# A routed feed-forward that gathers by an inverted list, first projections in two strands, and the next layer's first entry moved forward

## The chip, the cores and the metric

The kernel runs on one core of one Trainium2 chip. The engines of the core work side by side, each through its own queue of instructions in order: PE (matrix products into PSUM), DVE (elementwise work, scans, reductions), ACT (functions and copies), POOL (general work, and the issue of indirect transfers) and SP (issue of transfers). Semaphores order them. The metric is the time of one execution in microseconds (us). The median of three runs of the kernel before is 2760.29 us (2757.69 to 2765.39).

## The reference, cut to what matters

Two layers act on x of 8 batches × 512 tokens × 256 features, in 32-bit floats.

Layer 0 norms x to xn and adds two branches to x. The first is a recurrence over tokens. With dx the difference between a three-tap filter of xn and xn, five mixtures of xn and dx are projected to r, k, v, the gate g and the decay w. For 16 heads of 16 rows a state S of 16 × 16 is run over the tokens forwards and backwards:

```
S = exp(w)[:, None] * S + k[:, None] * v[None, :]      y_t = r_t S     (forwards)
y_t = r_t S;   S = exp(w)[:, None] * (S + k v)                         (backwards)
```

Both sums are gated, normed by head, multiplied by silu(g) and projected by Wo. The second branch is a mixture of 8 experts: each token's two best experts by score (xn Wg^T) compute silu(x W1^T) * (x W2^T) W3^T with 704 hidden values, and the two results are added with the scores as weights.

Layer 1 norms the sum, adds a global (causal) and then a local (window of 64) attention with 16 heads, and a feed-forward of 16 routed experts, four for each token out of two of four groups, beside a shared one.

## The kernel before, in words

**Layer 0, head.** `norm_and_route(b)` (L279) norms a batch, transposes it (xT), writes the transposed batch to DRAM (`lines`), and scores and picks its two experts. `projections(b)` (L480) loads the transposed batch (xnT), forms dx, and makes in one chain: the sigmoid gate (sig), the mixing factors (t5), the mixtures (`mixed`, L551, tile xf) and the projections v, k, r, d (decay), dq (what the two-sided scan multiplies by) and g. The product v goes to DRAM (vd). A plain loop adds the eight routings, two turns for each, and the first projections, entered up to three times in one turn. `clear_slots` (L272) writes zeros over all of `slots`, a DRAM table of 9984 rows of 1 KB (39 chunks of 256). `place` (L311) counts the picks of each expert, gives every pick a row in the table (`slot`), with chunks of 256 rows that belong to one expert, and names the expert of each chunk (`wrow`).

**Layer 0, scans.** `scans` (L674) goes through 128 steps (8 batches × 2 halves × 8 pairs of value rows). A step multiplies v, spread over partitions by eight transfers (`spread`, tile kv), by k (L688), runs two pairs of scans on DVE (L699, L703), multiplies by r (L708), and PE sums over rows (ys, L714). Beside it run the projections of the next batch, `ending` (L726: gate, norm, Wo, and the write of the batch to `after`), and the experts: `scatter` (L372) sends 4096 token rows twice to their slots by 64 indirect transfers from POOL, and `experts` (L410) goes through the 39 chunks: weights by indirect load (`weights`), the chunk's rows by a direct load (`load_slots`, L394), their transpose (xsT, L405), the products, and a write to `outs`.

**Layer 1.** `entry(b)` (L891) loads `after`, gathers for each token its two rows of `outs` (tile y, L903), adds them with weights (L911), norms, transposes, and routes. `heads_of`, `attentions`, `divided` and `ffn` do the attention and the feed-forward; the weights w1 of the feed-forward and of the projections are loaded at its start.

**What sets the order.** Every piece is a Python generator. `Turns.turn` advances each running generator by one step, so a `yield` says how far pieces are interleaved; scans have 4 steps for each of 128, a chunk of experts has 12. PE, DVE, ACT and SP keep this written order (`PINNED`); POOL's order is made by the scheduler. Tiles with one tag share buffers, and a new tile waits until the old one's readers are done.

Of the kernel before, what the change touches and what calls it, by code (L numbers as in the profile page):

```python
# [26 lines left out]
F32 = mybir.dt.float32  # L27
# [33 lines left out]
G1 = 4  # L61
# [13 lines left out]
for _n, _w in (  # L75
    ("ident", P), ("take", 32 + 24), ("mean", P), ("center", P), ("tri8", E0 * E0),
    ("before", P), ("fresh", E0 * NTT), ("full", T * B // CH), ("chunk", NCH), ("part", 1),
    ("tri16", E1 * E1), ("tri4", G1 * G1), ("causal", P), ("band", P + WIN),
    ("cos_g", NT * HD), ("sin_g", NT * HD), ("cos_l", NT * HD), ("sin_l", NT * HD),
):  # L80
    _C[_n] = (_at, _at + _w)
    _at += _w
# [4 lines left out]
def constants():  # L87
# [19 lines left out]
    put("chunk", np.arange(NCH)[None, :])  # L107
# [58 lines left out]
def two_layers(ctx: ExitStack, tc: tile.TileContext, a: dict, out: bass.AP):  # L166
# [6 lines left out]

    cst = const.tile([P, FIRST_L1], F32, name="cst")
# [6 lines left out]
    act_e.dma_start(wg0, a["wg0"])  # L181

# [23 lines left out]
    def layer_norm(dst, src, tag):  # L206
# [8 lines left out]
        rsqrt(rs, rs, NT)  # L215
        for t in range(NT):
            vec_e.tensor_scalar(
                dst[:, t, :], src[:, t, :], mv[:, t, 0:1], rs[:, t : t + 1], ALU.subtract, ALU.mult
            )

    def chosen(dst, s, n, k, tri, tmp, tag, tags=None):

        rows = s.shape[1]
        tags = tags or (f"gt{n}", f"eq{n}")
        gt = tmp.tile([P, rows, n, n], F32, tag=tags[0], name=f"gt{n}_{tag}", bufs=1)
        eq = tmp.tile([P, rows, n, n], F32, tag=tags[1], name=f"eq{n}_{tag}", bufs=1)
# [10 lines left out]


    with ExitStack() as l0:
# [3 lines left out]
        ew = l0.enter_context(tc.tile_pool(name="ew", bufs=2))  # L243
        hpool = l0.enter_context(tc.tile_pool(name="h0", bufs=4))
        ex = l0.enter_context(tc.tile_pool(name="ex", bufs=2))
# [20 lines left out]
        score = keep.tile([P, NTT, E0], F32, name="score")  # L266
        pick0 = keep.tile([P, NTT, E0], F32, name="pick0")
        slots = dram.tile([NSLOT, D], F32, name="slots", bufs=1)
        lines = [dram.tile([D, T], F32, name=f"xnT{b}", tag=f"xnT{b}", bufs=1) for b in range(B)]
        xns = [ex.tile([P, NT, D], F32, name=f"xn{b}", tag=f"xn{b}", bufs=1) for b in range(B)]  # L270

        def clear_slots():  # L272

            zero = rw.tile([P, D], F32, tag="t5a", name="zero")
            vec_e.memset(zero, 0.0)
            n = NSLOT // P
            nc.sync.dma_start(slots.rearrange("(p n) d -> p n d", p=P), bc(zero, 1, n))

        def norm_and_route(b):  # L279
            xn = xns[b]  # L280
            layer_norm(xn, xn, f"a{b}")
# [13 lines left out]
            ps = ps_rw.tile([P, T], F32, tag="rw", name=f"sc_{b}")  # L295
# [9 lines left out]
            chosen(pick0[:, b * NT : (b + 1) * NT, :], s, E0, TOP0, C["tri8"], rw, f"a{b}")  # L305
# [4 lines left out]

        def place():  # L311
            def tmp(shape, name, tag=None):
                return rw.tile(shape, F32, tag=tag or name, name=name, bufs=2 if tag == "gn" else 1)
# [9 lines left out]
            pe.matmul(ps[:, 1, :], one, flat(pick0), start=True, stop=True)  # L323

# [15 lines left out]
            vec_e.tensor_tensor(past, bc(C["chunk"], 2, E0), bc(chto, 1, NCH), ALU.is_ge)  # L340
# [4 lines left out]
            vec_e.tensor_copy(wrow, own)  # L345

# [17 lines left out]
            vec_e.tensor_copy(slot[1], high)  # L364
            vec_e.tensor_tensor(at, pos, bc(high, 2, E0), ALU.is_equal)
# [6 lines left out]
        def scatter():  # L372
            for n in range(NTT):
                for i in range(2):
                    put = pool_e.indirect_dma_start(
                        out=slots,
                        out_offset=bass.IndirectOffsetOnAxis(ap=slot[i][:, n : n + 1], axis=0),
                        in_=xns[n // NT][:, n % NT, :], in_offset=None,
                    )

                    tc.declare_no_dep(put.ins, group="scatter", query=mybir.DependencyQuery.ANY_SYNC, reason="slots are disjoint")
                    tc.add_to_no_dep_group("scatter", put.ins)
                yield

# [9 lines left out]
        def load_slots(i):  # L394
            xs = ex.tile([P, NS, D], F32, tag="xs", name=f"xs_{i}", bufs=2)
            pool_e.dma_start(
                xs, slots[i * CH : (i + 1) * CH].rearrange("(n p) d -> p n d", p=P)
            )
            return xs
# [10 lines left out]
        def experts():  # L410
            nxt = weights(0, "wgu", a["w0_gu"], GU0, 2)
            ps = turned(0, load_slots(0))
# [67 lines left out]
        def projections(b):  # L480

            xnT = rw.tile([P, NC, T + 2 * PAD], F32, tag="xnT", name=f"xnT_{b}")
            pool_e.memset(xnT[:, :, 0:PAD], 0.0)
            pool_e.memset(xnT[:, :, PAD + T :], 0.0)
            nc.sync.dma_start(
                xnT[:, :, PAD : PAD + T], lines[b].rearrange("(c p) t -> p c t", p=P)
            )
            xT = [xnT[:, c, PAD : PAD + T] for c in range(NC)]
            for _ in range(3):
                yield  # L490

            def shifted(c, s):
                return xnT[:, c, PAD + s : PAD + s + T]
# [7 lines left out]
            def project(w, xs, co, name):  # L501
# [8 lines left out]

            dx = big("dx", 1)
            for c in range(NC):
                o = dx[:, c, :]
                vec_e.tensor_scalar(o, xT[c], V("conv1", c), None, ALU.mult)
                vec_e.scalar_tensor_tensor(o, shifted(c, -1), V("conv0", c), o, ALU.mult, ALU.add)
                vec_e.scalar_tensor_tensor(o, shifted(c, 1), V("conv2", c), o, ALU.mult, ALU.add)
                yield
            dxs = [dx[:, c, :] for c in range(NC)]

            sig = big("sig")  # L520
            pss = []
            for co in range(NC):
                pss.append(project(5, dxs, co, f"gate{co}"))
                yield
            for co in range(NC):
                act_e.activation(sig[:, co, :], pss[co], AF.Sigmoid, bias=V("gate_b", co))
            xxx = []
            for c in range(NC):
                t = rw.tile([P, T], F32, tag="xf", name=f"xxx{c}_{b}", bufs=4)
                vec_e.scalar_tensor_tensor(t, dxs[c], V("maa_x", c), xT[c], ALU.mult, ALU.add)  # L530
                xxx.append(t)
# [3 lines left out]
            yield  # L535
            both = ((t5a, 0, 0, P), (t5b, P, 64, 96))
            pss = []
            for _, lo, r0, r1 in both:
                ps = bank(f"t5{lo}")
                for c in range(NC):  # L540
                    pe.matmul(
                        ps[r0:r1, :], m1w[:, c, lo : lo + r1 - r0], xxx[c],
                        start=c == 0, stop=c == NC - 1,
                    )
                pss.append(ps)
                yield
            for (t5, _, r0, r1), ps in zip(both, pss):
                act_e.activation(t5, ps[r0:r1, :], AF.Tanh)
            yield

            def mixed(*fs):  # L551

                xs = {f: [] for f in fs}
                for c in range(NC):
                    pss = []
                    for f in fs:
                        ps = bank(f"m{f}{c}")
# [8 lines left out]
                    for f, ps in zip(fs, pss):  # L566
                        t = rw.tile([P, T], F32, tag="xf", name=f"xf{f}{c}_{b}", bufs=4)
# [3 lines left out]

                        (vec_e if b < 2 else pool_e).tensor_tensor(t, t, xT[c], ALU.add)
# [5 lines left out]
            def projected(xs, w, name):  # L578

                pss = []  # L580
                for co in range(NC):
                    pss.append(project(w, xs, co, f"{name}{co}"))
                    yield
                return big(name), pss

            xv, xk = yield from mixed(2, 1)
            v, pss = yield from projected(xv, 2, "v")
            for co in range(NC):
                act_e.copy(v[:, co, :], pss[co])
            vd = dram.tile([D, T], F32, tag="vd", name=f"vd_{b}")  # L590
            act_e.dma_start(vd.rearrange("(c p) t -> p c t", p=P), v)
            yield


            k, pss = yield from projected(xk, 1, "k")
            for co in range(NC):
                act_e.mul(k[:, co, :], pss[co], -1.0)
            yield

            d = rw.tile([P, NC, T + 1], F32, tag="d", name=f"d_{b}", bufs=2)  # L600
            vec_e.memset(d[:, :, T:], 0.0)
            dT = d[:, :, :T]
            xw, xr = yield from mixed(0, 3)
            ps = bank("dw")
            for c in range(NC):
                pe.matmul(ps[:64, :], dw1[:, c, :], xw[c], start=c == 0, stop=c == NC - 1)
            yield
            act_e.activation(th[:64, :], ps[:64, :], AF.Tanh)
            r, pss = yield from projected(xr, 0, "r")
            for co in range(NC):  # L610
                act_e.copy(r[:, co, :], pss[co])
            pss = []
            for co in range(NC):
                pss.append(bank(f"w{co}"))
# [809 lines left out]
```

## Time and profile before

| what | value |
|---|---|
| median of three runs | 2760.29 us |
| the profiled execution's own time | 2747.16 us |
| its span, first to last instruction | 2745.4 us |
| PE, DVE busy | 2338.7 us (85%), 2141.9 us (78%) |
| ACT, POOL busy | 865.9 us (32%), 472.3 us (17%) |
| first product of the scans, last one's end | 144.86 us, 1443.7 us |
| first matmul of layer 1's feed-forward | 1513.5 us |
| HBM read and written | 215.17 MB, 45.88 MB |

A row of the profile's table of stretches gives the stretch, its length, and for PE, PE's weight loads, DVE, ACT and POOL the busy time with the number of instructions, then the granted clock of PE, the share of DMA and its GB/s. A row of the timeline gives the start, the time, the engine, the line, the operation and its tiles; in brackets stands the idle time before it and what ended it. A row of the waits gives who waited for whom: us in all, times, longest.

### The profile page before, as it was taken

To read this page: it belongs to the slowest core of one execution; us is meant where nothing else is said; L and a number is where in the kernel's file an instruction comes from. 1 tells how busy PE (TensorE), PEld (TensorE's weight loads), DVE (VectorE), ACT (ScalarE), POOL (GpSimd) and SP (SyncE) were. 2 spreads that over 40 slices of the span, in tenths; PEclk is the share of its full clock that TensorE was granted. 3 is DMA by queue.
4 is the path that set the end of the run, shared out by engine and by line. 5 is a ranking of instruction groups with operands and counts; after the bars stand their busy time and mean duration, and the time that the engine had idled before them with its cause. 6 is when DMAs were issued, how large, how long until landed. Compare 5 with 4: busy or idle time off the path is not lost. (4 is left out here: it accounts for less than half of the span.)

```text
span 2745.4 us, 32489 instructions
## 1 busy us (share of the span) xinstructions
PE 2338.7 (85%) x11772; PEld 1392.8 (51%) x11772; DVE 2141.9 (78%) x3042; ACT 865.9 (32%) x1649; POOL 472.3 (17%) x446
## 2 busy tenths in 40 slices
PE   4756897998989889898864899999989989998996
PEld 3313555555555555555632445555545545555554
DVE  4698989989999999999994857667576676666666
ACT  1303231232312323132111344444333444334344
POOL 0075132222223222132202110010010101001000
PEclk8767998989999999998986999999989999999998
DMA  8245555445454454545533100010010111000000
GB/s 286 77 147 167 149 162 163 132 135 158 157 174 133 140 161 142 175 153 153 174 87 140 55 28 24 9 45 21 16 32 32 31 32 31 22 26 20 20 9 16
DMA packets 108912, 263.23 MB, mean 96 GB/s; under 512 B 25265, under 2 KB 56401, under 8 KB 103633
## 3 DMA queue, kind: packets, MB, share of 16 engines
q1 hardware_dynamic: 76304, 119.35, 15.1%
q0 software_dynamic: 23616, 124.14, 13.9%
q10 hardware_dynamic: 8832, 17.65, 1.7%
q8 instruction: 95, 1.56, 0.2%
q14 instruction: 65, 0.52, 0.1%
HBM read 215.17 MB, written 45.88 MB: 95 GB/s over the span
## 5 line engine op out<-in xcount | busy, mean ns | idle before, releaser
L703 DVE TENSOR_TENSOR_SCAN kv<-d,kv 128x512 f32<-128x512 f32 x256 | 336.9, 1316 | 8.8
L699 DVE TENSOR_TENSOR_SCAN kv<-dq,kv 128x512 f32<-128x512 f32 x256 | 324.8, 1269 | 2.5
L426 PE MATMUL g<-xsT,wgu 128*128 128x256 f32 x936 | 248.0, 412 | 20.1 <-ACT xsT L418 19.6
L465 PE MATMUL y<-wdn,h 128*128 128x256 f32 x936 | 254.5, 410 | 8.7 <-DVE h L435 8.7
L1167 ACT ACTIVATE pt_g<-sc_g 128x512 f32<-128x512 f32 (+1 forms) x384 | 171.0, 532 | 236.4 <-PE sc_g L1159 201.7
L426 PEld LDWEIGHTS g<-xsT,wgu 128*128 128x128 f32 x936 | 188.3, 206 | 102.1 <-issue 38.6
L465 PEld LDWEIGHTS y<-wdn,h 128*128 128x128 f32 x936 | 170.8, 197 | 105.2 <-issue 73.7
L1261 PE MATMUL g<-xT,w 128*128 128x512 f32 x384 | 197.5, 639 | 24.8 <-DVE h L1296 9.4
L1261 PE MATMUL u<-xT,w 128*128 128x512 f32 x384 | 190.7, 620 | 18.7 <-DVE h L1296 7.6
L714 PE MATMUL ys<-kv,cst 128*32 128x512 f32 x512 | 123.2, 653 | 79.0 <-DVE kv L708 78.8
L426 PE MATMUL u<-xsT,wgu 128*128 128x256 f32 x780 | 189.3, 382 | 0.0
L1307 PE MATMUL y<-w,h 128*128 128x256 f32 x768 | 179.3, 385 | 0.0
L426 PEld LDWEIGHTS u<-xsT,wgu 128*128 128x128 f32 x780 | 148.2, 191 | 36.2 <-issue 14.0
L708 DVE TENSOR_TENSOR kv<-kv,r 128x1024 f32<-128x1024 f32 x128 | 160.2, 1251 | 3.7
L1279 DVE TENSOR_TENSOR h<-h,u 128x512 f32<-128x512 f32 x96 | 66.0, 688 | 123.6 <-PE u L1261 119.0
L688 DVE TENSOR_TENSOR kv<-kv,k 128x1024 f32<-128x1024 f32 x128 | 160.2, 1251 | 0.0
L1307 PEld LDWEIGHTS y<-w,h 128*128 128x128 f32 x768 | 141.7, 190 | 32.2 <-issue 9.5
L452 ACT ACTIVATE h<-g 128x512 f32<-128x512 f32 (+1 forms) x117 | 61.5, 526 | 300.6 <-PE g L426 300.3
L1173 DVE TENSOR_TENSOR pt_g<-pt_g,cst 128x512 f32<-128x512 f32 x128 | 85.2, 686 | 69.7 <-ACT pt_g L1167 69.6
L1167 ACT ACTIVATE pt_l<-sc_l 128x384 f32<-128x384 f32 (+1 forms) x256 | 98.0, 470 | 90.9 <-PE sc_l L1159 72.9
L1261 PEld LDWEIGHTS g<-xT,w 128*128 128x128 f32 x384 | 71.4, 199 | 107.2 <-issue 82.6
L903 POOL DMA_INDIRECT y<-outs,slot x64 | 64.7, 1010 | 324.8 <-DVE acc L911 312.6
(298 smaller groups left out, 3858.9 us busy)
## 6 DMA issues: line engine op xcount, KB each, us to landing
kv<-vd SPq DMA_DIRECT2D x1024, 64.0 KB, 2.4
cb<-cd SPq DMA_DIRECT2D x128, 128.0 KB, 2.9
slots<-zero SPq DMA_DIRECT2D x1, 9984.0 KB
xs<-slots POOLq DMA_DIRECT2D x39, 256.0 KB, 7.2
outs<-ys POOLq DMA_DIRECT2D x39, 256.0 KB, 5.7
w<-in_w ACTq DMA_DIRECT2D x12, 384.0 KB, 9.7
xn<-in_x SPq DMA_DIRECT2D x8, 512.0 KB
xnT<-xT ACTq DMA_DIRECT2D x16, 256.0 KB, 2.0
```

Of the source, the lines that this page charges most:

```text
L426: pe.matmul(o, w[:, at + c * P : at + (c + 1) * P], xT[:, c, :], start=c == 0, stop=c == NC - 1,)
L465: pe.matmul(y[:, n, :], hs[j // 2][lo:, j % 2, n * P : (n + 1) * P], wd[lo:, j * D : (j + 1) * D], start=j == 0, stop=j == NJ0,)
L688: vec_e.tensor_tensor(kv, kv, bc(kc, 1, NV), ALU.mult)
L699: vec_e.tensor_tensor_scan(out=kv[:, i, :], data0=qc, data1=kv[:, i, :], initial=0.0, op0=ALU.mult, op1=ALU.add,)
L703: vec_e.tensor_tensor_scan(out=kv[:, i, ::-1], data0=dc[:, ::-1], data1=kv[:, i, ::-1], initial=0.0, op0=ALU.mult, op1=ALU.add,)
L708: vec_e.tensor_tensor(kv, kv, bc(rc, 1, NV), ALU.mult)
L714: pe.matmul(y[r0 : r0 + 32, :], C["take"][:, 24 - 8 * at : 56 - 8 * at], kv[:, i, :], start=at == 0, stop=at == 3, skip_group_check=True,)
L1167: act_e.activation(pt[:, i, :end], scs[i][:, :end], AF.Exp, scale=0.25)
L1173: vec_e.tensor_tensor(pt[:, :, a0 : a0 + m], pt[:, :, a0 : a0 + m], bc(mask[:, :m], 1, 4), ALU.mult,)
L1261: pe.matmul(ps, w[:, k, c * P : (c + 1) * P], xT[:, c, :], start=c == 0, stop=c == NC - 1,)
L1279: vec_e.tensor_tensor(hs[-1], hs[-1], u, ALU.mult)
L1307: pe.matmul(y[:, i, :], hs[k][:, (t + i) * P : (t + i + 1) * P], w1[j - 5 + k][:, 2, :], start=k == 0, stop=k == 5,)
```

## The change

- **The table by gather.** `clear_slots`, `slots` and `scatter` go. `norm_and_route` writes the normed batch as it is to a DRAM tensor `normed`, eight transfers of 512 KB on SP's queue. `turn_round` makes from `slot` the inverse list `whose` (which token stands in a row of the table): each slot is split into its low seven bits and the rest, DVE compares both with a count (128 × 512 and 128 × 312 elements at a time), ACT scales one of the two by the token's number, and 64 matmuls add all up in PSUM. `load_slots` then gathers a chunk's 256 rows from `normed` by two indirect transfers. Rows without a pick get token 0.
- **Place beside the scans.** `place`, `turn_round` and `experts` are one generator that starts with the scans.
- **Two strands.** `projections` returns three generators: `inputs` (dx, t5), `values` (sig, v, k) and `decays` (r, d, dq, then g). For batch 0 the last two run side by side, the second with PSUM banks and tiles of its own; the head ends when k and dq are ready, and g comes after. For the other batches they run one after the other. The add of xn in `mixed` is POOL's for all batches (before: DVE's for batches 0 and 1).
- **The first entry.** When the experts are done, `begin` gives their SBUF space to the weights of layer 1 (w1, gq, go, lqkv), loads them, and starts `entry(0)` beside the last scans. `entry` and its helpers move ahead of layer 0, its tiles into a pool `hold` that both layers share (xn lies there first, then the comparisons of `turn_round`).

```
-        slots = dram.tile([NSLOT, D], F32, name="slots", bufs=1)
+        normed = dram.tile([B * T, D], F32, name="normed", bufs=1)
...
         def norm_and_route(b):
             xn = xns[b]
-            layer_norm(xn, xn, f"a{b}")
+            yield from layer_norm(xn, xn, f"a{b}")
+            nc.sync.dma_start(tokens(normed[b * T : (b + 1) * T]), xn)
             yield
...
-        def scatter():
-            for n in range(NTT):
-                for i in range(2):
-                    put = pool_e.indirect_dma_start(
-                        out=slots,
-                        out_offset=bass.IndirectOffsetOnAxis(ap=slot[i][:, n : n + 1], axis=0),
-                        in_=xns[n // NT][:, n % NT, :], in_offset=None,
-                    )
...
+        def turn_round():
...
+            for k in range(NTT // 4 + 1):
+                if last:
+                    for j in range(4):
+                        for i in range(2):
+                            pe.matmul(
+                                inv, last[0][:, i, j, :], last[1][:, i, j, :],
+                                start=k == 1 and i + j == 0,
+                                stop=k == NTT // 4 and (i, j) == (1, 3),
+                            )
+                    last = None
+                if k < NTT // 4:
+                    ls = held(k % 4, [P, 2, 4, P], f"ls{k}")
+                    hs = held(4 + k % 4, [P, 2, 4, n2], f"hs{k}")
+                    for i in range(2):
+                        for o, of in ((ls, low), (hs, high)):
+                            n = o.shape[3]
+                            vec_e.tensor_tensor(
+                                o[:, i], bc(of[i][:, 4 * k : 4 * k + 4], 2, n),
+                                bc(C["count"][:, :n], 1, 4), ALU.is_equal,
+                            )
+                    for j in range(4):
+                        n = 4 * k + j
+                        act_e.activation(
+                            hs[:, :, j, :], hs[:, :, j, :], AF.Copy, scale=number[:, n : n + 1]
+                        )
+                    last = ls, hs
+                yield
+            vec_e.tensor_copy(whose, inv)
...
         def load_slots(i):
             xs = ex.tile([P, NS, D], F32, tag="xs", name=f"xs_{i}", bufs=2)
-            pool_e.dma_start(
-                xs, slots[i * CH : (i + 1) * CH].rearrange("(n p) d -> p n d", p=P)
-            )
+            for n in range(NS):
+                at = i * NS + n
+                pool_e.indirect_dma_start(
+                    out=xs[:, n, :], out_offset=None, in_=normed,
+                    in_offset=bass.IndirectOffsetOnAxis(ap=whose[:, at : at + 1], axis=0),
+                )
...
-        first = projections(0)
+        start, values, decays = projections(0)
+        beside = [start, values, decays]
         for b in range(B):
             turns.add(norm_and_route(b))
+            if 2 <= b < 8:
+                turns.add(beside[{2: 0, 3: 0, 4: 2, 5: 1, 6: 2, 7: 1}[b]])
             turns.turn()
-            if b == 1:
-                turns.add(first)
-                turns.turn()
-                clear_slots()
-            elif b in (2,3):
-                turns.add(first)
+        while ("scans", 0) not in done:
             turns.turn()
-        for _ in range(3):
-            turns.turn()
-        place()
-        turns.finish()
-        turns.add(then(scatter(), experts()))
+        def begin():
+            side.close()
+            pool = ctx.enter_context(tc.tile_pool(name="w1", bufs=1, side="right"))
+            yield
...
+            turns.add(entry(0))
+            for _ in range(6):
+                yield
...
+            for j in range(NF1):
+                w1.append(pool.tile([P, 3, D], F32, name=f"w1_{j}", tag=f"w1_{j}"))
+                act_e.dma_start(w1[j], a["w1"][j])
+                yield
...
+        slot_work = then(place(), turn_round(), experts(), last())
+        turns.add(slot_work)
         for _ in scans(turns):
             turns.turn()
         turns.finish()
```

## The prediction

> **What bounds the kernel now.** I read first the busy tenths over the span, then the busy time by stretches that I cut at the ends of the stages, then the waits and the order of instructions at the three seams. The stretches (columns: PE, PE weight load, DVE, ACT, POOL busy, then granted clock, DMA share, GB/s):
>
> ```profile
> 0.00:144.86 144.86, 84.39 (x272) 49.32 (x272) 85.10 (x232) 30.65 (x43) 12.93 (x21) 0.80 0.54 183
> 144.86:236.00 91.14, 48.00 (x96) 13.89 (x96) 88.53 (x90) 15.16 (x21) 72.26 (x64) 0.69 0.43 148
> 236.00:249.00 13.00, 7.97 (x28) 5.38 (x28) 1.60 (x3) 4.82 (x6) 3.40 (x4) 0.68 0.65 232
> 249.00:1421.00 1172.00, 1040.46 (x4037) 654.28 (x4036) 1107.29 (x1096) 303.32 (x477) 282.36 (x236) 0.95 0.51 152
> 1421.00:1443.70 22.70, 5.69 (x12) 0.52 (x12) 22.28 (x19) 0.00 (x0) 0.77 (x1) 0.52 0.03 12
> 1443.70:1513.50 69.80, 28.93 (x90) 17.29 (x91) 28.62 (x70) 10.40 (x19) 17.38 (x20) 0.62 0.39 138
> 1513.50:1600.00 86.50, 74.29 (x336) 38.87 (x336) 69.49 (x155) 29.94 (x60) 18.24 (x18) 0.92 0.20 59
> 1600.00:2650.00 1050.00, 976.27 (x6142) 563.11 (x6141) 681.09 (x1290) 427.37 (x920) 62.97 (x82) 0.97 0.08 25
> ```
>
> Three bounds follow each other. The head (to 144.86, the first product of the scans) is a chain: DVE works 85 of 145 us. The scan stage (144.86 to 1443.7, 1298.8 us) is DVE's: 97%, then 94%, then 98% busy. Layer 1 from 1513.5 on is PE's, 93% busy. Between lies a seam of 70 us where nobody works half the time. Two stalls stand in the head and at the first expert chunk (waits from 20 to 145 us; then DVE's and PE's instructions in order):
>
> ```profile
> DVE xf L568 <- PE m L561: 17.5, 3, 15.3
> ...
> ACT t5a L548 <- DMA slots<-zero: 10.6, 1, 10.6
> ```
> ```profile
> 236.12 1.21 DVE L688 TENSOR_TENSOR kv<-kv,k 128x1024 f32<-128x1024 f32 x1
> 248.73 0.75 DVE L568 SCALAR_TENSOR_TENSOR xf<-m,vecs,dx 128x512 f32<-128x512 f32 x1 [11.40 <-PE m L563]
> ```
> ```profile
> 241.03 1.11 PE L405 MATMUL xsT<-cst,xs 128*128 128x128 f32 x4 [17.66 <-DMA xs<-slots]
> ```
>
> The tanh waits until the 10 MB clear has read its source tile; and at 236 the matmul that DVE needs stands in PE's queue behind the transpose of the first gathered chunk, which waits for all 64 scatters. The last seam, in PE's order:
>
> ```profile
> 1460.04 1.99 PE L777 MATMUL o<-wmix,z 128*128 128x256 f32 x8 [0.78 <-DVE x L782]
> 1490.93 2.25 PE L858 MATMUL x<-cst,x 128*128 128x128 f32 x8 [28.89 <-DVE x L926]
> ...
> 1513.50 3.62 PE L1261 MATMUL g<-xT,w 128*128 128x512 f32 x4
> ```
>
> PE has no work of layer 1 until entry(0) has gathered, normed and routed.
>
> **What the skill says.** The Trainium skill, SBUF — State Buffer, "SBUF: two separate sides": DVE and GpSimd share one port pair by an exclusive lock, which a DVE instruction with two SBUF inputs also takes against a GpSimd operation that reads SBUF. The trace agrees: the POOL add of L572 runs from 1.08 to 2.14 us (median 1.92), and the scan of L703, 1.225 at the median, reaches 2.11. The skill, Perfetto Trace Analysis, "Sequencer Loop": an instruction waits in its engine's queue for its semaphores; the 17.66 us above is such a wait, with everything behind it late. The skill, DMA: Bandwidth & Descriptors, "Anatomy of one DMA": about 2.0 us plus bytes over 436 GB/s, so 2.3 us for 128 rows of 1 KB; the trace has 2.8 for y<-outs,slot, which I use.
>
> **The change part by part.** Sums are against the profiled execution (span 2745.4, time 2747.2); the median of the runs shown, 2760.3, stands 13.1 us above it, and I carry the difference over to that median.
>
> 1. Head. place() leaves it: DVE's first instruction of it that waited is at 133.90, the first product at 144.86. The clear leaves it (from 47 to 59 DVE did nothing: 12 us). The gather's source is written by eight 512 KB writes of xn on SP's queue, each waiting for its norm; the load of xnT stands behind two of them, whose norms end near 16 us, before its own data (about 19): no cost. The two strands overlap the values' matmuls with the decays' chain. I walked DVE's new order with old durations: norm statistics 2.4 us a batch, norm 1.4, choice 2.6, dx 2.0 a half, xxx 1.4. Up to 20 us nothing changes (the first xT copy waits for ACT's table at 15.3, the first score for that). From there DVE has, before the strand's first xf: norms 2 to 6, statistics 3 to 6, choices 0 to 3, dx and xxx, together 5×1.4 + 4×2.4 + 4×2.6 + 5.4 = 32.4, so xf near 52; with statistics 7, choice 4 and four xf of 0.74 the fourth ends near 60. The adds go to POOL: four at 1.9 end near 64. Then dw 1.9, tanh 0.6, sc, r, xt, r and v on PE (about 10), w 2.3, table load and exponentials 3.6, so q begins near 81; q 1.9, logarithm and exponential with two loads 5.0 behind the copies of v (about 88); dq 5.1, k 1.2: first product near 94 by full-clock matmuls. (Its kv: vd issued near 83, 3.0 to land, eight issues of 0.45 and 2.4 to land, 92; SP's last normed write, ahead of them, waits only for norm 7 near 62.) The granted clock was 0.57 to 0.64 in parts of the old head; I add 6 for it: **100**, so **−45** (−55 to −35). Check from the other side: the old chain without place (−15), clear (−12) and the g input (−3) gives 115, and the strands must hide some 15.
> 2. place() on DVE beside the scans, which DVE bounds: **+11** (133.90 to 144.86 without a gap). The first strand's xf of g after the first product: **+1.5**.
> 3. turn_round: 16 comparisons 128x512, 16 of 128x312, 9 small. The rows 128x512 (L228) are 0.69 long and start 0.60 to 0.72 apart; 128x312 (L340) is 0.48. 16×0.65 + 16×0.46 + 1.9 = **+19.7** (17 to 24). Its 64 matmuls and 32 ACT scalings lie where PE is 53% and ACT 17% busy: hidden; uncovered, each group of eight would hold DVE for about 2 us.
> 4. The 64 scatters (POOL busy 73 us) go, and with them the 11.4 us stall; list and first gather can leave a stall of 0 to 8, I take 4: **−7.4**. Each chunk has two indirect gathers of about 1.3 us on POOL instead of one direct issue of 0.74; POOL is 24% busy and its new order has the gathers two chunks ahead: nothing. If that lead went, PE would wait as at 241. On POOL the first gather waits for the list, and adds of batch 1 queue behind it; batch 1's scans need those only some hundred us later.
> 5. Batch 1's ten adds go from DVE (0.69 each) to POOL: −6.9, given back in part by the shared lock: **−5**.
> 6. entry(0) moves into the last 25 turns of the scans, where DVE is full: 8 accumulations 3.9, statistics and norm 3.9, routing 13.2: **+21**. Its gathers wait for the last chunk's outs (5.7 us to land), then 1.3 apart and 2.8 to land, with a second group behind the first; DVE's accumulations stand ahead of the last scans, which stand still with them: the ys copy to the fourth landing is 0.6 + 0.8 + 5.7 + 3×1.3 + 1.0 + 2.8 = 15 us, DVE's own work in between about 12; the second group needs 8 and finds 4. So 7, and 1 for routing behind ACT's weight issues: **+8** (0 to 18).
> 7. Layer 1. Old: scans end 1443.7, last issue of layer 0 at 1462.8, lat at 1496.95, first scores at 1546.9. New: constants and gdown still load only when layer 0 lets go (19 us after the scans), so lat about 24 us after the scans, not 53; from lat to the first scores 50 us of PE work stand in the new order (before: 50 us elapsed), and I allow 5 for waits. Scores come 24 us earlier, and ffn(0) is about 14 us of matmuls further then. The end of PE's order is the same, so part of that lead is lost: **−30** (−42 to −18). Loads of w1, gq, go and lqkv on ACT's queue lie in a stretch of 12 GB/s: nothing.
>
> Sum: −45 + 11 + 1.5 + 19.7 − 7.4 − 5 + 21 + 8 − 30 = **−26**; the median 2760.3 becomes 2734.
>
> **Rivals.** *A, the chains pack better* (chance 0.24): first product at 90, no tail stall, the whole lead kept (−39): −26 −10 −8 −9 = −53, 2707. For it: the old layer 1 loses 12 us of PE in 1513 to 1600. Against: PE, not DVE, sets the strand after 65. *B, the pull-forward is given back* (0.12): attention sets layer 1's end and the lead dissolves, −30 becomes −12: −8, 2752. For it: both orders end alike, with attention alone. *C, slower* (0.14): gathers hold PE. The transposes of a chunk stand ahead of ys and projection matmuls in PE's queue; if a gather is late by more than 0.7 us in each of 39 chunks (27 us), the gain is gone; late by 1.3 gives +25, 2785. For it: five software DMAs a chunk instead of four, with the lock. Against: old xs landed in 7.2 us, and a chunk lasts some 30. That the change does not do what it says is no case: the order shows place beside the scans.
>
> **How the numbers follow.** A run tells a change from none at about 0.3% (8 us). The main case has 0.5 and its own range 2714 to 2752. Faster: 0.47 of it, all of A, 0.03 of B: 0.74. Within: 0.03 and 0.07: 0.10. Slower: C and 0.02 of B: 0.16. The range from 2700 to 2772 takes in main, most of A, B and a mild C.
>
> **What would show it.** Right: first kv<-kv,k near 100; no waits of 10 us on DVE before it or at the first xsT; scans of about 1350 us with DVE still over 95%; lat_g about 24 us after the last kv. Wrong: PE waits on xs in many chunks; DVE waits of over 10 us on y<-outs or on decays' exponentials; first product later than 115; scores no earlier than 95 us after the scans.

## The result and the profile after

The changed kernel takes 2766.9 us (median of 18 runs, 2763.7 to 2771.5), the kernel before 2757.8 (18 runs, 2750.7 to 2765.4): ratio 1.0033, 95% interval 1.0025 to 1.0040. It is slower by a third of a per cent, where 26 us less were predicted. The profiled executions are further apart, 2769.7 against 2745.4 us of span: before's took 2747.2 us, less than any of the 18 timed runs, and after's 2771.5, the most of its 18. So the stages compared below sum to 24 us where the medians say 9.

Busy time by stretches of the kernel after, cut at the first product of the scans, at the starts of batches 1 and 7, at the end of the scans and at the first scores of layer 1 (columns: PE, PE weight load, DVE, ACT, POOL, then granted clock, DMA share, GB/s):

```profile
0.00:96.86 96.86, 71.07 (x262) 43.80 (x262) 67.78 (x188) 28.06 (x40) 18.64 (x23) 0.90 0.52 179
96.86:290.10 193.24, 150.06 (x568) 91.06 (x568) 180.91 (x220) 48.12 (x89) 56.75 (x44) 0.83 0.43 126
290.10:1321.00 1030.90, 912.21 (x3408) 561.96 (x3408) 939.94 (x934) 274.37 (x422) 308.33 (x242) 0.92 0.50 147
1321.00:1484.00 163.00, 91.75 (x364) 56.20 (x364) 146.51 (x176) 20.56 (x35) 22.92 (x19) 0.76 0.48 134
1484.00:1573.60 89.60, 66.23 (x198) 36.91 (x198) 52.45 (x114) 19.14 (x32) 19.64 (x21) 0.77 0.20 62
1573.60:2769.70 1196.10, 1089.48 (x7105) 630.33 (x7104) 764.25 (x1436) 492.19 (x1066) 73.82 (x92) 0.95 0.08 24
```

The kernel before, cut at the same points of its work (its head, 0.00:144.86, stands in the prediction's table):

```profile
144.86:308.80 163.94, 107.17 (x344) 53.99 (x346) 148.83 (x149) 30.77 (x47) 87.81 (x79) 0.80 0.48 157
308.80:1310.10 1001.30, 894.85 (x3403) 554.59 (x3400) 940.37 (x934) 270.22 (x419) 251.25 (x209) 0.94 0.50 151
1310.10:1443.70 133.60, 100.11 (x427) 65.48 (x425) 130.49 (x125) 22.31 (x39) 19.73 (x16) 0.91 0.45 133
1443.70:1546.90 103.20, 54.89 (x159) 29.35 (x159) 53.74 (x124) 18.69 (x32) 27.04 (x29) 0.69 0.35 119
1546.90:2745.40 1198.50, 1097.33 (x7173) 640.05 (x7172) 783.34 (x1483) 493.24 (x1070) 73.54 (x93) 0.96 0.08 25
```

Stage by stage: the head is 48.0 us shorter. The first batch is 29.3 longer, the last 29.4, layer 1 16.0 shorter: all four were in the sum. Batches 1 to 6 were not. The sum left them alone, and they take 1030.9 us instead of 1001.3, although DVE works the same 940 us in both, in the same 934 instructions. DVE stands still for 91 us instead of 61. Its waits in these batches, after (total, times, longest):

```profile
DVE h L615 <- PE u L606: 18.0, 12, 2.9
DVE z L961 <- PE rs L959: 17.6, 8, 3.0
...
DVE x L978 <- PE o L973: 11.2, 10, 2.9
...
DVE xf L727 <- PE m L720: 8.1, 8, 2.1
```

and before, where z hardly waits at all:

```profile
DVE x L782 <- PE o L777: 7.2, 6, 2.5
DVE xf L568 <- PE m L561: 6.3, 5, 2.3
DVE h L435 <- PE u L426: 5.1, 5, 2.5
...
DVE z L765 <- PE rs L763: 1.4, 2, 0.7
```

Four different products of PE are late by 1 to 3 us each time. PE's own waits in the same batches have one row that the kernel before doesn't have, the first line here; the second is a row of the kernel before that the kernel after doesn't have:

```profile
PE t L761 <- DVE xxx L753: 28.0, 6, 7.3
```
```profile
PE gate L505 <- DVE dx L516: 9.6, 6, 2.0
```

So the products that wait for DVE at this point changed: t for xxx in place of the gate for dx, and three times as long.

### The profile page after: what moved, and what is told of

The parts are those of the page before. It is cut to its first block, busy times and chain, and to the rows that moved or that the text cites. A ratio compares the mean times of both kernels' runs of the same rounds, so it can differ in the third digit from the quotient of the medians.

```text
span 2769.7 us, 32796 instructions
## 1 busy us (share of the span) xinstructions
PE 2380.8 (86%) x11900; PEld 1420.3 (51%) x11900; DVE 2151.8 (78%) x3063; ACT 882.4 (32%) x1684; POOL 500.1 (18%) x441
## 4 chain that ended last, share of the span: by engine, by line
PE 55%; DVE 28%; issue 7%; DMA 4%; ACT 3%; SPq 2%; POOL 1%; DVEq 0%; ACTq 0%; POOLq 0%
PE y L1404 6%; PE g L1358 5%; PE u L1358 4%; DVE kv L895 4%; PE g L606 4%; PE y L645 4%; PE u L606 3%; DVE kv L899 3%; PE sc_g L1256 2%; DMA kv<-vd 2%; PE o_g L1284 2%; DVE kv L884 2%; PE ys L910 2%; PE t L761 2%; PE qkv_l L1148 2%
## 5 line engine op out<-in xcount | busy, mean ns | idle before, releaser
L645 PE MATMUL y<-wdn,h 128*128 128x256 f32 x936 | 261.8, 419 | 12.1 <-DVE h L615 11.3
L606 PE MATMUL g<-xsT,wgu 128*128 128x256 f32 x936 | 236.7, 398 | 27.9 <-ACT xsT L598 24.2
L645 PEld LDWEIGHTS y<-wdn,h 128*128 128x128 f32 x936 | 176.7, 203 | 112.8 <-issue 70.0
L1358 PE MATMUL g<-xT,w 128*128 128x512 f32 x384 | 205.5, 662 | 26.9 <-DVE att_l L1312 14.0
L606 PE MATMUL u<-xsT,wgu 128*128 128x256 f32 x780 | 204.0, 403 | 0.0
L904 DVE TENSOR_TENSOR kv<-kv,r 128x1024 f32<-128x1024 f32 x128 | 167.0, 1305 | 2.4
L1404 PEld LDWEIGHTS y<-w,h 128*128 128x128 f32 x768 | 144.4, 194 | 34.3 <-issue 11.2
L730 POOL TENSOR_TENSOR xf<-xf,xnT 128x512 f32<-128x512 f32 x80 | 117.0, 1481 | 237.3 <-DVE xf L727 237.0
```

The costliest lines, as they stand in the source:

```text
L606: pe.matmul(o, w[:, at + c * P : at + (c + 1) * P], xT[:, c, :], start=c == 0, stop=c == NC - 1,)
L645: pe.matmul(y[:, n, :], hs[j // 2][lo:, j % 2, n * P : (n + 1) * P], wd[lo:, j * D : (j + 1) * D], start=j == 0, stop=j == NJ0,)
L730: pool_e.tensor_tensor(t, t, xT[c], ALU.add)
L904: vec_e.tensor_tensor(kv, kv, bc(rc, 1, NV), ALU.mult)
L1358: pe.matmul(ps, w[:, k, c * P : (c + 1) * P], xT[:, c, :], start=c == 0, stop=c == NC - 1,)
L1404: pe.matmul(y[:, i, :], hs[k][:, (t + i) * P : (t + i + 1) * P], w1[j - 5 + k][:, 2, :], start=k == 0, stop=k == 5,)
```

## The experiments

Below, "idle" is the sum of DVE's gaps of over 0.25 us in batches 1 to 6 (44.7 us before, 75.2 after), and "wait for xxx" is the row just shown, in the same batches. Names with a_ are the kernel after with an edit, those with b_ the kernel before with one. Times are medians. Every ratio is to the kernel before, from runs of it beside these on the same chip. The idle time has a scatter of its own: kernels whose edits don't touch these batches lie up to 7 us apart (after 75.2, a_entry1 72.4, a_nolist 68.3; a_sig 43.5, a_sig_sp 38.5, a_sig_heads 39.4), so smaller differences of it are not read.

| kernel | time, us | ratio, 95% interval | idle | wait for xxx |
|---|---|---|---|---|
| before | 2757.8 | | 44.7 | none |
| after | 2766.9 | 1.0033 (1.0025 to 1.0040) | 75.2 | 28.0 |
| a_m1 | 2748.4 | 0.9961 (0.9948 to 0.9973) | 49.0 | 17.7 |
| a_p1 | 2748.7 | 0.9957 (0.9935 to 0.9980) | 55.1 | 23.0 |
| a_p2 | 2740.5 | 0.9931 (0.9913 to 0.9949) | 56.2 | 24.6 |
| b_p1 | 2747.3 | 0.9962 (0.9948 to 0.9976) | 39.4 | none |
| a_direct | 2764.0 | 1.0015 (1.0001 to 1.0030) | 69.8 | 27.7 |
| a_nolist | 2751.0 | 0.9964 (0.9951 to 0.9977) | 68.3 | 27.4 |
| a_entry1 | 2764.5 | 1.0014 (0.9996 to 1.0031) | 72.4 | 28.3 |
| a_sig | 2735.0 | 0.9907 (0.9876 to 0.9938) | 43.5 | none |
| b_p1_sig | 2772.9 | 1.0052 (1.0032 to 1.0072) | 67.1 | 26.1 |
| a_xxx | 2745.2 | 0.9950 (0.9935 to 0.9966) | 50.7 | 9.5 |
| a_sig_p2 | 2726.1 | 0.9875 (0.9834 to 0.9915) | 42.5 | none |
| a_sig_sp | 2728.8 | 0.9894 (0.9864 to 0.9924) | 38.5 | none |
| a_sig_heads | 2722.0 | 0.9860 (0.9828 to 0.9893) | 39.4 | none |
| a_all | 2720.3 | 0.9867 (0.9852 to 0.9883) | 43.1 | none |
| a_all_p2 | 2718.2 | 0.9840 (0.9820 to 0.9860) | 42.5 | none |

**First: is it where the chunks fall?** DVE's gaps after repeat every three batches. A chunk takes 12 turns and a batch 64, so the two meet in the same way every third batch, and the turn at which the first chunk starts decides how. A step of the scans has four turns; the texts below count where a chunk starts by the remainder of its turn by 4. The edit, with 2, 4 and 5:

```diff
             xs = load_slots(0)
-            for _ in range(3):
+            for _ in range(2):
                 yield
             ps = turned(0, xs)
```

> The kernel after, with two empty turns instead of three ahead of the first chunk's transposes, so that every chunk stands one turn earlier against the scans' turns (chunk i begins at turn 17+12i instead of 18+12i; before it was 33+12i, the same remainder by 4 as 17). Theory 'alignment' (the 29 us of new DVE idle time in batches 1 to 6 come from where the chunks' turns fall against the scans' four-turn steps): idle in batches 1 to 6 falls from 75 to about 45 us, the time from 2767 to about 2738 (2730 to 2745). Theory 'gathers' (the idle time comes from the two indirect gathers of each chunk and the shared port): the time stays at 2767 within 6, the idle time within 6 of 75.

> The kernel after with four empty turns there (chunk i at 19+12i), a third remainder by 4. Alignment: the idle time of batches 1 to 6 takes a value of its own, repeating every three batches, anywhere from 40 to 90 us, and the time follows it one to one from 2767 - (75 - idle). Gathers: 2767 within 6.

> The kernel after with five empty turns there (chunk i at 20+12i), the fourth remainder by 4. Alignment: again an idle time of its own between 40 and 90 us and a time that follows it. Gathers: 2767 within 6.

> The kernel before, with one empty turn more between the scatters and the first chunk (chunk i at 34+12i: the remainder that the kernel after has). Nothing else differs. Alignment: DVE's idle time in batches 1 to 6 rises from 44.5 to about 75 us, the time from 2758 to about 2787 (2780 to 2793). Gathers: 2758 within 6, since this kernel has no gathers.

One empty turn more or less is worth 18 us, two more 26: the placing matters, and no gather was touched. The time doesn't follow the idle time one to one: a_m1 has the least idle of the three (49.0), but at 2748 lies above the range expected of it, and a_p2 with 56.2 is the fastest. The better placings keep 18 to 25 us of the wait for xxx and still lose a quarter to a third of the idle time. In a_p2 the 18.0 us of h waiting for u are gone from DVE's waits, while z waits for rs as long as in the kernel after:

```profile
DVE z L961 <- PE rs L959: 18.7, 6, 5.0
```

Why one placing is better than another was not followed further. But the theory as written falls with b_p1. The placing that was to cost the kernel before 29 us saves it 11, so the remainder by 4 is not what carries the loss. Something else in the kernel after makes its own placing a bad one.

**Second: gathers, list, entry or gate?** In batches 2 to 7 the projections of the two kernels differ in one thing (batch 1 also in its adds): the gate's product (sig) stood ahead of xxx and the tanh's matmuls t, and stands behind them now. It came with the cut into strands, by which batch 0 alone starts its values and decays beside each other. a_sig moves it back for batches 1 to 7:

```diff
                     yield
+                if not first:
+                    sig, pss = yield from projected(dxs, 5, "sig")
...
                 xxx = []
...
-                sig, pss = yield from projected(dxs, 5, "sig")
+                if first:
+                    sig, pss = yield from projected(dxs, 5, "sig")
...
```

The other three of the group: a direct load in place of the gathers, turn_round without its work, and entry(0) left in layer 1.

```diff
-            for n in range(NS):
-                at = i * NS + n
-                pool_e.indirect_dma_start(
...
+            pool_e.dma_start(
+                xs, normed[i % 16 * CH : (i % 16 + 1) * CH].rearrange("(n p) d -> p n d", p=P)
+            )
```
```diff
-            inv = ps_e.tile([P, n2], F32, tag="e", name="inv")
...
-            vec_e.tensor_copy(whose, inv)
+            for _ in range(NTT // 4 + 1):
+                yield
+            for at in range(0, n2, NTT):
+                n = min(NTT, n2 - at)
+                vec_e.tensor_copy(whose[:, at : at + n], number[:, :n])
```
```diff
-            turns.add(entry(0))
...
-            then(*(entry(b) for b in range(1, B))), then(*(ffn(b) for b in range(B))),
+            then(*(entry(b) for b in range(B))), then(*(ffn(b) for b in range(B))),
```

> The kernel after, with the gate's projection (sig) of batches 1 to 7 moved back to where the kernel before has it, ahead of the tanh and not behind it; the number of turns is the same and all later turns of a batch's projections stay where they are. Theory 'queue order': this is the one difference that is left in PE's order of a batch besides the chunks' placing, so idle in batches 1 to 6 falls from 75 towards the 39 that the kernel before has with this placing, and the time to about 2735 to 2750. Theory 'gathers': nothing, 2767 within 6.

> The kernel after, but each chunk fetches 256 consecutive rows of the normed tokens by one direct DMA on the same queue instead of two gathers by the list (this leaves the gathering out: the chunks work on other tokens; list and turns stay). Theory 'gathers' (what the four placings of the chunks have in common, some 59 us of DVE idle time in batches 1 to 6 against 42 in the kernel before, is the price of the two gathers and of POOL's longer queue): idle in batches 1 to 6 falls by about 17 us and the time to about 2750. Theory 'queue order' (it comes from what else stands in PE's order and from the granted clock, not from how the rows arrive): idle stays at 75 within 8, the time at 2767 within 8.

> The kernel after with the 32 comparisons, 32 scalings and 128 matmuls of turn_round left out (the list is then a plain count, so the chunks gather other tokens); its turns and the gathers stay. The prediction's price for it: 19.7 us of DVE less 0.6 for three small copies, so the first batch falls from 193 to about 174 us and the time to about 2748. Rival: PE's matmuls and the 5.6 us that DVE waits for m at 156 to 166 come on top, and the time falls by about 25, to 2742.

> The kernel after with entry(0) left in layer 1, first in its turns as in the kernel before, while the weights of layer 1 are still loaded in the last turns of the scans. By the prediction's parts 6 and 7 as measured (29 us in the last batch, about 30 in layer 1) the two cancel: the last batch falls from 163 to about 134 us if entry(0) is the cause of all of it, layer 1 grows by about 30, and the time stays at 2767 within 6. Rival, 'the loads': the 7.9 us in which kv waits for its DMA at 1415 come from the weight loads and stay, so the last batch falls to only about 142 and the time rises to about 2775.

a_sig takes 32 us off and brings the idle time to 43.5, before's value. DVE's waits in its batches 1 to 6, of which z for rs was 17.6 and h for u 18.0:

```profile
DVE h L615 <- PE u L606: 11.2, 7, 2.9
...
DVE z L968 <- PE rs L966: 4.3, 2, 2.8
```

a_direct leaves time and idle nearly where they were: by the medians the two gathers cost 3 us (2764.0 to 2766.9), by intervals that overlap, and 69.8 us of idle lie within the scatter. The gathers, the prediction's rival C, are out as the cause of the loss. a_nolist shortens the first batch from 193.2 to 174.0 us, 19.2, and the time by 16.

How the gate's place works is seen in PE's order at the start of batch 2. After:

```profile
474.65 1.46 PE L645 MATMUL y<-wdn,h 128*128 128x256 f32 x6
479.98 3.31 PE L761 MATMUL t<-xxx,m1w 128*128 128x512 f32 x4 [3.87 <-DVE xxx L753]
483.09 2.06 PE L645 MATMUL y<-wdn,h 128*128 128x256 f32 x6
485.08 1.90 PE L761 MATMUL t<-xxx,m1w 128*32 128x512 f32 x4
486.91 0.66 PE L959 MATMUL rs<-cst,wide 128*128 128x128 f32 x4
```

and DVE, which wants that rs:

```profile
487.61 0.69 DVE L961 TENSOR_TENSOR z<-z,rs 128x512 f32<-128x512 f32 x1 [2.02 <-PE rs L959]
```

The same stretch of a_sig:

```profile
471.68 1.46 PE L645 MATMUL y<-wdn,h 128*128 128x256 f32 x6
472.97 1.88 PE L685 MATMUL sig<-dx,wmix 128*128 128x512 f32 x4
474.69 1.65 PE L645 MATMUL y<-wdn,h 128*128 128x256 f32 x6
476.91 0.66 PE L966 MATMUL rs<-cst,wide 128*128 128x128 f32 x4 [0.57 <-ACT sig L753]
...
480.23 1.88 PE L766 MATMUL t<-xxx,m1w 128*128 128x512 f32 x4
```

PE reaches the matmuls t before DVE has made xxx, and stops for 3.87 us. Then come t (3.31 us where it takes 1.88 in a_sig), an expert's y, more t, and behind all of them rs, for which DVE waits. In a_sig the gate's matmuls fill that time. Their input dx is ready or nearly so: in batches 1 to 6 they wait 8.4 us for it, 2.0 at most. When t comes up its input is there, and rs has passed already. In each of the six batches of the kernel after, DVE's next gap behind PE's wait for xxx, some 8 us later, is a wait for rs; these six make 12.0 us. The other waits that grew (h for u, x for o, xf for m) lie farther off, and only the runs tie them to the gate.

**Third: does the move alone do it, also in the kernel before?** b_p1 with the gate moved back behind the tanh:

```diff
-            sig = big("sig")
+            if b == 0:
+                sig = big("sig")
...
             for (t5, _, r0, r1), ps in zip(both, pss):
                 act_e.activation(t5, ps[r0:r1, :], AF.Tanh)
             yield
+            if b > 0:
+                sig = big("sig")
...
```

> The kernel before with its chunks one turn later (as in b_p1), and the gate's projection of batches 1 to 7 moved behind the tanh, to where the kernel after has it; the number of turns is the same. Theory 'queue order' (the gate's move makes the idle time): idle in batches 1 to 6 rises from 39 in b_p1 to about 70 to 75 us, mostly as z waiting for rs, x for o, h for u and xf for m, and the time from 2747 to about 2778. Rival (the move costs only together with the gathers, the list's matmuls or the other banks of the kernel after): 2747 within 8.

It costs 25.6 us (2747.3 to 2772.9), in a kernel with scatters and without list, gathers or strands; idle rises to 67.1, a little less than expected. Its waits in batches 1 to 6 have the same rows as those of the kernel after, on PE and on DVE:

```profile
PE t L543 <- DVE xxx L532: 26.1, 6, 7.3
```
```profile
DVE z L775 <- PE rs L773: 14.9, 7, 3.4
DVE h L436 <- PE u L427: 13.4, 6, 2.9
```

**Fourth: the wait or the place?** a_xxx leaves the gate behind the tanh and gives DVE one turn more for xxx, taken from the empty turns at a batch's start:

```diff
-                for _ in range(3):
+                for _ in range(3 if first else 2):
                     yield
...
                     xxx.append(t)
                 yield
+                if not first:
+                    yield
```

> The kernel after, gate behind the tanh, where batches 1 to 7 have one empty turn between making xxx and the tanh's matmuls, and one fewer at their start, so that all later turns stay. Theory 'the wait for xxx' (the tanh's matmuls come to the head of PE's queue before DVE has made xxx, and what stands behind them, rs, o, u and m, is late): PE's 28 us of waits of t for xxx fall below 8, idle in batches 1 to 6 from 75 to 40 to 50, the time from 2767 to 2735 to 2742, as in a_sig. Rival 'the gate's place' (its own eight matmuls beside those of the tanh crowd rs and o): the wait goes, idle stays above 60, the time above 2752.

```profile
PE t L763 <- DVE xxx L753: 9.5, 2, 4.8
```
```profile
DVE z L963 <- PE rs L961: 4.0, 2, 2.5
```

The wait falls by 18.5 us, z's wait for rs by 13.6, idle by 24.5 and the time by 21.7, of the 32 that a_sig gains. All three numbers miss what the first theory expected by a little (9.5 for under 8, 50.7 for 40 to 50, 2745 for 2735 to 2742), and lie off the rival's. So with the gate left in its place, about two thirds of the loss come back when xxx is there earlier. What is left goes with the 9.5 us and with the gate's place itself; these two are not told apart. Nor is the wait a price by itself: the edit also moves dx and xxx one turn earlier in DVE's order, and a_p2 gains 26 us with 24.6 us of the wait left.

**Fifth: what the other edits are worth.** The last batch has a wait that belonged to nothing in the prediction, here after:

```profile
DVE kv L884 <- DMA kv<-vd: 7.9, 1, 7.9
```

With entry(0) gone (a_entry1) it does not go, it grows; DVE in order:

```profile
1412.16 1.23 DVE L884 TENSOR_TENSOR kv<-kv,k 128x1024 f32<-128x1024 f32 x1 [8.80 <-DMA w<-in_w]
...
1426.75 1.23 DVE L884 TENSOR_TENSOR kv<-kv,k 128x1024 f32<-128x1024 f32 x1 [5.16 <-DMA kv<-vd]
```

It is the loads of layer 1's weights. ACT, with nothing ahead of them, issues gq, go, lqkv and the first w1 within 2 us, in the kernel after from 1405.3 to 1407.1, in a_entry1 from 1401.4 to 1403.1. SP, which issues the parts of each kv, then stands before many of these issues until a load of w1 (w) has landed; its waits in a_entry1 from 1400 to 1427:

```profile
SPq L861 <- DMA w<-in_w: 15.0, 11, 2.7
```

So the next kv come late, and the last batch shrinks by 16.9 us only; the rival had expected about 21. But the time does not rise by 8, since layer 1 grows by 10.1 and not by 30. a_sig_sp issues them on SP's queue, where the scans' own loads pace them; a_sig_heads makes entry(1) and ffn(0) wait for the first block's heads; a_sig_p2 is a_sig with the chunks two turns later.

```diff
-                act_e.dma_start(W[name], a[of])
+                nc.sync.dma_start(W[name], a[of])
...
-                act_e.dma_start(w1[j], a["w1"][j])
+                nc.sync.dma_start(w1[j], a["w1"][j])
```
```diff
-            then(*(entry(b) for b in range(1, B))), then(*(ffn(b) for b in range(B))),
+            then(until("heads", 0), *(entry(b) for b in range(1, B))),
+            then(until("heads", 0), *(ffn(b) for b in range(B))),
```

> a_sig with the loads of layer 1's large weights (gq, go, lqkv and w1) issued on SP's queue, one a turn between the scans' own loads, instead of on ACT's, which issues four of them within 2 us. Theory 'the loads': the wait of 8.1 us for kv in the last batch falls below 2 us and the time by about 7, to 2728. Rival (the wait is entry(0)'s, whose acc load and gathers are in the same stretch): 2735 within 3, the wait stays.

> a_sig with entry(1) and ffn(0) of layer 1 held back until the first block's heads are made. Theory 'the lead is lost in front of the first scores' (64 us lie between lat and the first scores, since entry(1) and ffn(0) stand in DVE's and PE's order between them, and attention's length sets the end): the first scores come 20 to 30 us earlier and the time falls by 10 to 25, to 2710 to 2725. Rival (what is held back has to be done later on a PE that is 93% busy): scores earlier, the time at 2735 within 5.

> a_sig (the kernel after with the gate ahead of the tanh) with the chunks two turns later, the placing that was best with the gate behind the tanh. Theory 'two separate costs' (the placing gives 26 us whatever the gate does): about 2710. Theory 'one cost' (both edits remove the same coincidences in PE's queue, so the second finds little left): 2735 within 8, idle in batches 1 to 6 at 35 to 50 us.

In a_sig_sp the 8.1 us for kv are gone from the last batch, whose first row of waits is now:

```profile
DVE acc L294 <- DMA y<-outs,slot: 4.8, 3, 2.1
```

The batch takes 158.7 us instead of 163.1. That the wait was the loads' is shown; the time falls by 6 in the medians, and the intervals overlap. a_sig_p2 finds nothing in batches 1 to 6 (42.5 us idle against 43.5), so the gains of placing and gate don't add. They are not the same waits, though: a_sig keeps 11.2 us of h for u, and a_sig_p2 has none of these but 10.6 of z for rs. With the gate ahead of the tanh every placing that was run, in either kernel, has 38.5 to 44.7 us of idle, with the gate behind it 49.0 to 75.2. The 9 us of a_sig_p2 against a_sig are within what the two intervals allow; the last batch, with 5.9 instead of 8.1 us of waiting for kv, gives 4 of them.

Layer 1 of a_sig and of a_sig_heads, from the last scan to the first scores and on to the end:

```profile
1448.50:1538.00 89.50, 65.05 (x194) 36.73 (x194) 52.38 (x113) 19.25 (x32) 20.25 (x21) 0.77 0.20 62
1538.00:2733.60 1195.60, 1087.85 (x7105) 630.39 (x7104) 764.07 (x1436) 492.19 (x1066) 73.91 (x92) 0.96 0.08 24
```
```profile
1443.50:1497.40 53.90, 30.60 (x90) 17.88 (x90) 19.19 (x35) 12.66 (x21) 8.96 (x12) 0.62 0.15 47
1497.40:2722.10 1224.70, 1117.72 (x7213) 649.09 (x7212) 797.58 (x1515) 497.47 (x1077) 83.59 (x102) 0.96 0.08 26
```

The first scores come 35.6 us earlier, and 29.1 of it are given back, for PE has the held-back matmuls still to do (1117.7 us of work instead of 1087.9). What stays is 6.5; the median fell by 13, by intervals that just overlap. Two more profiles bear the smaller figure out: layer 1 takes 1274.5 to 1281.8 us in the three kernels with this edit (a_sig_heads, a_all, a_all_p2) and 1279.9 to 1288.7 in those with the order of the kernel after.

**Sixth: together.** a_all has gate, loads and heads; a_all_p2 also the placing.

> The kernel after with three edits: the gate ahead of the tanh, layer 1's large loads on SP's queue, and entry(1) and ffn(0) held until the first heads are made. If the gains add (32, 6 and 6 to 13): 2715 to 2723. If the last two find the same time: 2728.

> a_all with the chunks two turns later. If the placing's gain of 9 (a_sig_p2 against a_sig) adds: 2706 to 2714. If it came from the last batch alone, where the loads no longer hold kv: equal to a_all within 4.

Both beat both kernels: 2720.3 and 2718.2, 1.3 to 1.6% below the kernel before. a_all lies in the range in which the three gains add; but between the two, and against a_sig_heads at 2722.0, the intervals don't separate. By the medians, gate and heads hold nearly all of the gain, and a_all_p2 is equal to a_all within 4 us, so no gain of the placing shows here.

## Why the prediction was wrong

The step that failed first is one that the sum doesn't have. Batches 1 to 6 of the scan stage were taken as unchanged because DVE's work there is unchanged, which is true to half a microsecond. The order on PE was not looked at for any batch but the first. The part on the head speaks of two strands that overlap "the values' matmuls with the decays' chain" and stops at batch 0, while the same lines of code run for all eight and move the gate from ahead of xxx to behind the tanh. That is +29.6 us in the profile; moving the gate back takes 32 us off the median. The prediction's own sign for being right, scans of about 1350 us with DVE over 95% busy, fails here: they take 1387 us with DVE 91% busy.

Two more terms were mis-sized. By the profiled executions the kernel is 24 us longer, so the sum of -26 misses by 50: batches 1 to 6 are 29.6 of it, layer 1 is 14.0 (item 7) and the first batch 9.5 (items 2 to 5), while the head was better by 3. By the medians, +9 against -26, the miss is 35.

By the prediction's numbers:

1. Head: 100 predicted, 96.86 measured, -48.0 instead of -45. Right. The two rows of 17.5 and 10.6 us are gone.
2. to 5., the first batch: +11, +1.5, +19.7, -7.4 and -5 make +19.8; measured +29.3, with DVE's work up 32.1 and its idle time down 2.8 (12.3 against 15.1). The list's price is right (19.2 in a_nolist against 19.7). place() runs between 102.5 and 117.6, its rows adding up to 11.4. Of the old stall of 11.4 us, 5.6 remain, as two waits of 4.5 and 1.1 for m. Half of the miss is again the gate: the projections of batch 1 run here, and PE's m waits 4.1 us for ACT to be done with the gate behind the tanh, while in a_sig 1.6 of the 5.6 are left and the batch takes 188.4 us instead of 193.2. The adds that went to POOL give nothing, where 5 was put. They took 6.9 us of DVE, and the 96 instructions of the scans in this batch (all that write kv) take 125.0 us together instead of 118.2. In the kernel before the same 96 take 118.2 in its first batch, where the adds beside them are DVE's, and 123.8 in the second, where they are POOL's. Two scans beside such adds at 161 to 165 took 1.68 and 1.93 us instead of 1.22. That the gathers cost next to nothing holds, by a_direct.
6. The last batch: +29 predicted, +29.4 measured, for partly wrong reasons, so the match is luck. entry(0)'s own DVE work is 19.3 us (146.5 us busy in this batch against 127.2 in a_entry1), near the 21. The stall is not that of entry's gathers, which wait 1.3 us; most of it is the weight loads that step 7 put down as "nothing".
7. Layer 1: -30 predicted, -16.0 measured. lat_g comes 25.6 us after the last kv, against 24 predicted, but from there to the first scores it takes 64 us and not 55: entry(1) and ffn(0) stand in between on DVE and PE. With both held back (a_sig_heads) these are 28 us. So the first scores come 13.6 us earlier after the scans, not 24. Moreover, an early start is worth little by itself (6.5 of 35.6 us in a_sig_heads). a_entry1, with the weights preloaded and entry(0) in layer 1, has a layer 1 of 1295.8 us; so entry(0)'s move gains 10.1 there and costs 16.9 in the last batch, and leaving it out changes the median by -2.4, which is within the intervals. Rival B, the pull-forward given back, described this part well.

The slower rival C named a wait in PE's queue with everything behind it late, on the wrong input: xs never holds PE, xxx does. That its break-even of 27 us lies so near the 28.0 of this wait is luck.

## What to carry to other kernels

When a generator is cut up or reordered for one iteration, list the new order on every in-order engine for all the iterations, also where its work is the same. A matmul whose input a full engine makes just one turn earlier needs other ready work ahead of it in the queue. Taking that away cost about as much as the wait itself here (28.0 us of wait and 32 us of time, 26.1 and 25.6 in b_p1_sig), though PE is not the engine that bounds the stage; with another placing of the chunks it cost about half of that (2740.5 in a_p2 against 2726.1 in a_sig_p2). An engine with the same busy time and longer gaps points to its supplier's queue: look there for the row that is new.

## What the runs showed of the hardware

A wait of PE can be followed by work at half the granted clock, which makes what stands behind it later still. In the kernel after, while PE is busy without a break:

```profile
390.00:395.00 5.00, 5.00 (x12) 3.37 (x10) 4.87 (x7) 2.36 (x3) 0.00 (x0) 0.50 1.00 248
...
400.00:405.00 5.00, 5.00 (x9) 2.14 (x8) 4.93 (x6) 0.00 (x0) 1.93 (x1) 0.50 0.00 0
```

and the same group of matmuls there and in b_p1 at the same place of the pattern, where the granted clock is 1.00:

```profile
406.36 3.78 PE L606 MATMUL g<-xsT,wgu 128*128 128x256 f32 x8 [1.16 <-ACT xsT L598]
```
```profile
585.30 1.99 PE L427 MATMUL g<-xsT,wgu 128*128 128x256 f32 x8 [1.16 <-ACT xsT L419]
```

Some 13 to 17 us ahead of both groups stands a wait of PE for yg, of 3.84 us in the one and 3.83 in the other. The Trainium skill, TensorE: Matmul & The Clock Gate, "What's actually happening": the clock falls to half after an idle window of about 3.4 us, and the windows run freely. The trace agrees for the stretch right after the gap, and equal gaps that end differently fit windows that run freely. It doesn't explain the second stretch of 0.50, from 400 to 405, ahead of which PE had been busy for over 10 us; that stays open. How much of the 29.6 us is this doubling and how much the waits themselves was not separated.
